# Feed-forward weights fetched one block in advance up to block 10, two from there on

## Chip, cores and metric

The kernel runs on one core of a Trainium2 chip. The metric is the device time of one execution in microseconds (us). The kernel before took 796.46 us (median of 3 runs, 795.83 to 797.32).

## What is computed

The input x has the shape (4, 1024, 256), in float32 as everything here. A transformer block is modulated by rows computed from a small conditioning input. First a gated linear recurrence takes the place of attention. Then a mixture of 8 experts follows, of which each token uses the best two:

```python
h = _layernorm(x) * (1 + ca) + sa
x = x + ga * attn(h)          # projections, sigmoid gates, a scan along the sequence, W_out
h = _layernorm(x) * (1 + cb) + sb
gate = softmax(h @ Wg + bg)   # 8 scores for each token; the two best, normalized
for e in range(8):
    y = gelu(h @ W1[e] + b1[e]) @ W2[e] + b2[e]
    output += y * combine_w[..., e]
x = x + gb * output
```

W1[e] is 256 x 1024 and W2[e] is 1024 x 256, so one expert's two matrices are 2 MB.

## The kernel before

**Chunks.** The first part runs over 8 chunks (NCH) of 512 tokens. In each, `project` (L417 for its matmuls) makes the four projections of one quarter of the hidden width, four times. Work of the neighbouring chunks is put between. A chunk's x1 is stored to the output (`o_resid`, L470), its second norm to a table `hx` in device memory (`f_store`, L498), and a swapped copy goes out and back for the router (`f_swap`, L518 and L525). For each batch of 1024 tokens the router ranks the tokens of every expert. `drain` (L586, on POOL) scatters (token, weight) pairs into `lists`, one region for each expert; a batch takes 16 scatters.

**Blocks.** The second part works through blocks of 256 entries of one expert. Which expert and which entries block j has is read from a small table computed on the chip (`entry`, L810). The table is made in three tiers. Blocks 0 to 7 (NE is 8) hold tokens of the first two batches, and blocks 8 to 15 (up to NM, 16) need three batches scattered. For each block there are these steps:

- `fetch_entries` (L822, on SP): 2 KB of the list, into `ent` (for the first 8 blocks `ente`).
- `fetch_rows` (L830, on POOL): two indirect gathers of 128 rows of `hx` each, into `hb`. They wait for the entries.
- `fetch_weights` (L852 to L855, on SP): four loads, which are w1 (1 MB), bb (4 KB), w2 (1 MB) and b2b (128 KB).
- `b_turn` (L911, on DVE): turns the rows into xT. Only for block 0 PE does it (L903), and this is put inside the last projection of the last chunk.
- `b_up` (L924, with the gelu on ACT, L933): 16 matmuls, which the trace shows as 32. `b_down` (L954): as many. DVE then adds the bias and multiplies (L968, L969), and POOL adds the rows to the output (L941).

**Buffers.** Weights have three places, used in turn: two sets of tiles, and for every third block the memory of the projection weights (`proj`, with b2b in `wo_sb`). So the weights of block j can start to load when block j - 3 is done with its own: w1 after its b_up, w2 after its b_down. Entries of block 8 and later have five places, and a place is free when its block's rows have been added to the output.

**Order.** The order on every engine is that of the program (a manual schedule); each engine runs ahead on its own until it meets a wait. All loads and stores of this part are issued by SP, one after another. SP waits at an instruction whose buffer is not free or whose data are not there, and everything behind it in the program waits too. So the place of a call in the program is a place in SP's queue.

**Where the change lies.** In the last chunk, after the second projection, the code calls `fetch_weights(0)`, `fetch_weights(1)`, then `fetch_entries` for blocks 0 to 7 (L1055 to L1063), and then on POOL the gathers of blocks 0 and 1. `fetch(j)` is called at the head of block j's work: L1116 for block 0, L1131 for block 1, L1160 for the later ones. It fetches entries of block j + 3 (from block 9 on), and rows and weights of block j + 2. The entries of the first block of a tier (8 and 16) are fetched two blocks in advance instead, and wait for all scatters of the batches in that tier (L1163). `fetch_used` does the same for the last blocks, of which the number is known only on the chip.

Of the kernel before, what the change touches and what calls it, by code (L numbers as in the profile page):

```python
# [19 lines left out]
def tile_adaln_block(  # L20
# [54 lines left out]
    NJ = (2 * T + E * (TK - 1)) // TK  # L75
# [3 lines left out]
    NE, EARLY_B, _ = TIERS[0]  # L79
# [48 lines left out]
    def load_x(c_: int, eng):  # L128
        xb = deep.tile([P, TPB, D], F32, tag="x", name=f"x_{c_}", bufs=5)
        b, i = divmod(c_, NB)  # L130
        src = x[b].rearrange("(n p) d -> p n d", p=P)
        eng.dma_start(out=xb, in_=src[:, ts(i, TPB), :])
        X[c_] = {"x": xb}
# [92 lines left out]
    def shift(c_):  # L226
        mv, rstd = X[c_]["stats"]
        nmr = small.tile([P, TPB], F32, tag="nmr", name=f"nmr_{c_}")
        X[c_]["nmr"] = nmr
        nc.vector.scalar_tensor_tensor(nmr, mv[:, :, 0], -1.0, rstd, ALU.mult, ALU.mult)  # L230
# [9 lines left out]
    def a_norm(c_):  # L240
        X[c_]["h"] = deep.tile([P, TPB, D], F32, tag="h", name=f"h_{c_}")
        norm(X[c_]["h"], c_)
# [116 lines left out]
    def a_mod(c_):  # L359
        h, md = X[c_]["h"], MDA[c_ // NB]  # L360
        nc.vector.tensor_mul(h, h, wide_row(md[:, 1, :]))
        nc.vector.tensor_add(h, h, wide_row(md[:, 0, :]))
# [112 lines left out]
    def f_stats(c_):  # L475
        X[c_]["stats"] = stats(X[c_]["x"], f"f{c_}")
# [105 lines left out]
    def drain(n: int):  # L582
        for _ in range(min(n, len(waiting))):
            nc.gpsimd.memset(between, 0.0)
            place, what = waiting.pop(0)
            ins = nc.gpsimd.indirect_dma_start(  # L586
                out=lists[:, :],
                out_offset=IndirectOffsetOnAxis(ap=place, axis=0),
                in_=what,
                in_offset=None,  # L590
                bounds_check=E * T - 1,
                oob_is_err=False,
            )

            for other in scattered:
                tc.declare_no_dep(ins.ins, other.ins, reason="other places")
            scattered.append(ins)
# [191 lines left out]
    def turns(pool, n: int, shape, dtype, tag: str, j: int):  # L789

        slots = kept.setdefault(tag, [None] * n)
        if slots[j % n] is None:
            slots[j % n] = pool.tile(shape, dtype, tag=f"{tag}{j % n}", name=f"{tag}_{j % n}", bufs=1)
        return slots[j % n]
# [6 lines left out]
    def seen(j: int):  # L801

        return next((batches * S for n, batches, _ in TIERS if j < n), T)

    def entry(j: int, row: int, most: int):
        which, i = next(
            ((w, j - n) for n, w in ((NM, "l"), (NE, "m"), (0, "e")) if j >= n)
        )
        what = tab[which]
        return nc.values_load(  # L810
            what[0:1, row, i : i + 1], engines=[SP], min_val=0, max_val=most,
            skip_runtime_bounds_check_because=why,
        )

    def fetch_entries(j: int):
        at = entry(j, 1, E * BPE)
        if j < NE:
            ent = xpool.tile([P, HK, 2], I32, tag=f"ente{j}", name=f"ente_{j}", bufs=1)
        else:
            ent = turns(xpool, 5, [P, HK, 2], I32, "ent", j)  # L820
        with nc.allow_non_contiguous_dma(reason="pairs of a list"):
            ld = nc.sync.dma_start(out=ent, in_=by_block[at])  # L822
        BK.setdefault(j, {}).update(ent=ent, ld=ld, gathers=[], acc=[])

    def fetch_rows(j: int, half: bool = False):

        hb = turns(xpool, 3, [P, HK, 2 * D], F32, "hb", j)
        for t in range(1 if half else HK):
            BK[j]["gathers"].append(
                nc.gpsimd.indirect_dma_start(  # L830
                    out=hb[:, t, :], out_offset=None, in_=hx[: seen(j), :],
                    in_offset=IndirectOffsetOnAxis(ap=BK[j]["ent"][:, t, 0:1], axis=0),
                    bounds_check=seen(j) - 1, oob_is_err=False,
                )
            )
        BK[j]["hb"] = hb

    def fetch_weights(j: int):
        if j >= NJ:
            return  # L840
        wpool = pools["w"]
        e = entry(j, 0, E - 1)
        if j % 3 == 2:
            w1 = proj[:, : KC * F].rearrange("p (k f) -> p k f", k=KC)
            w2 = proj[:, KC * F :].rearrange("p (c d) -> p c d", c=FC)
            b2b = wo_sb[:, 0, :]
        else:
            w1 = turns(wpool, 2, [P, KC, F], F32, "w1", j % 3)
            w2 = turns(wpool, 2, [P, FC, D], F32, "w2", j % 3)
            b2b = turns(wpool, 2, [P, D], F32, "b2b", j % 3)  # L850
        bb = turns(wpool, 3, [P, FC], F32, "bb", j)
        nc.sync.dma_start(out=w1, in_=W1r[e])  # L852
        nc.sync.dma_start(out=bb, in_=b1d[e])
        nc.sync.dma_start(out=w2, in_=W2r[e])
        nc.sync.dma_start(out=b2b, in_=b2[ds(e, 1), :].broadcast_to((P, D)))  # L855
        BK.setdefault(j, {}).update(w1=w1, w2=w2, bb=bb, b2b=b2b)
# [4 lines left out]
    def fetch(j: int):  # L861

        if j + 2 in firsts:
            fetch_entries(j + 2)
        if NE < j + 3 < NJ and j + 3 not in firsts:
            fetch_entries(j + 3)
        if j + 2 < NJ:
            fetch_rows(j + 2)
            fetch_weights(j + 2)

    def fetch_used(j: int, half: bool):
# [144 lines left out]
    for c_ in range(NCH):  # L1016
        nxt, prv, old = c_ + 1, c_ - 1, c_ - 2
        more, was, been = nxt < NCH, prv >= 0, old >= 0
        b, part = divmod(c_, NB)

        route = old // NB if been and old % NB == NB - 1 else None
        placed = (c_ - 3) // NB if c_ >= 3 and (c_ - 3) % NB == NB - 1 else None


        if c_ + 3 < NCH:
            load_x(c_ + 3, nc.sync)
        if more:
            shift(nxt)
        project(c_, 0, [lambda: a_norm(nxt)] if more else [])
        drain(6 if c_ + 2 >= NCH else 3)  # L1030
        if more:
            a_mod(nxt)
        if was:
            a_skip(c_)
            o_pe(prv)
            o_resid(prv)
        if placed is not None:
            r_second(placed)
        if part == NB - 1:
            load_mdf(b + 1)  # L1040


        if part == 0 and was:
            scale_out(b)
        if was:
            f_stats(prv)
        project(c_, 1, [lambda: a_square(nxt)] if more else [])
        if c_ == 0:
            first_contents()
        drain(6 if c_ + 2 >= NCH else 3)  # L1050
        if placed is not None:
            r_rank_pe(placed)
        if been:
            f_gate(old)
        if not more:  # L1055
            fetch_weights(0)
            fetch_weights(1)
            for j in range(NE):
                fetch_entries(j)

            wait_for(BK[0]["ld"], scattered)
            fetch_rows(0)
            fetch_rows(1)  # L1063
        if part == 0:
            if c_ == 0:
                setup_ctx.close()
                pools["w"] = ctx.enter_context(tc.tile_pool(name="weights", bufs=2))
            load_gb(b)
            load_mda(b + 1)
        elif c_ == 1:  # L1070
            clear_rows()
            if c_ == 0:
                load_mdf(1)


        if more:
            a_root(nxt)
        if was:
            shift(prv)
        if placed is not None:  # L1080
            r_place(placed)
        if route is not None:
            r_softmax(route)
        if more:
            a_scale(nxt)
        project(
            c_, 2,
            ([lambda: f_norm(prv)] if was else [])
            + ([lambda: r_exp(route)] if route is not None else []),
        )  # L1090
        drain(6 if c_ + 2 >= NCH else 3)
        if part == 0:
            store_gb(b)
        if c_ + 2 < NCH:
            a_stats(c_ + 2)


        if not was:
            a_skip(c_)
            scale_out(b)  # L1100
        if was:
            f_mod(prv)
            f_store(prv)
        project(c_, 3, [lambda: a_turn(nxt) if more else b_turn(0)])
        drain(6 if c_ + 2 >= NCH else 3)
        if was:
            f_swap(prv)
        if route is not None:
            r_first(route)
        if placed == EARLY_B - 1:  # L1110
            tab["e"] = full_table(NE, "e")
# [129 lines left out]
```

## Time and profile before

| | |
|---|---|
| median of 3 runs | 796.46 us |
| the profiled execution | 795.87 us, span 794.1 us |
| PE (TensorE matmul) busy | 773.7 us, 97% of the span |
| DVE (VectorE) busy | 504.7 us, 64% |
| POOL (GpSimd) busy | 292.7 us, 37% |
| ACT (ScalarE) busy | 242.1 us, 30% |
| DMA | 138.13 MB, mean 174 GB/s |
| granted TensorE clock, mean | 0.992 |

The profile is of one execution. Times in it count from the start of the span. PEld is the loading of weights into TensorE, which goes on beside the matmuls. Queue names with a q at the end (SPq, POOLq) are the engine's own instruction queue, in which it issues DMAs. "Idle before" is the time that an engine stood before an instruction, with what ended it. "To landing" is the time from a DMA's issue until its data are there.

From the span's start to about 308 us PE works on the projections, and from 308 us on it works on blocks, first mixed with the last work of the first part and from 347 us without it. The costliest groups of PE are those of the blocks:

```profile
L954 PE MATMUL pye_False<-w,g_False 128*128 128x256 f32 x672 | 148.7, 379 | 0.0
L924 PE MATMUL ph_False<-xT,w 128*128 128x256 f32 x672 | 148.6, 379 | 0.0
...
L924 PE MATMUL ph_False<-xT,proj 128*128 128x256 f32 x320 | 70.7, 379 | 0.0
L954 PE MATMUL pye_False<-proj,g_False 128*128 128x256 f32 x320 | 70.7, 379 | 0.0
```

One of these rows gives line, engine, operation, output and inputs, shape and count; after the bar come the busy us in all and the mean ns of one; after the next bar the idle us before them. The weights are moved by these issues (KB each, median us to landing):

```profile
w<-in_L_ffn_W_dram SPq DMA_DIRECT2D x48, 1024.0 KB, 7.0
proj<-in_L_ffn_W_dram SPq DMA_DIRECT2D x24, 1024.0 KB, 7.4
```

### The profile page before, as it was taken

Reading aid. Unit: us, or ns where it says so; the run is one execution under the profiler, and the core shown is the slowest. Engines: PE = TensorE matmul, PEld = TensorE weight load, DVE = VectorE, ACT = ScalarE, POOL = GpSimd, SP = SyncE. Lnnn points to the kernel's source line nnn. Section 1 sums busy time; section 2 is a strip of 40 time slices with the busy share of each in tenths; the row PEclk is TensorE's granted clock in tenths of the full one; section 3 lists DMA queues with packets and bytes.
Section 4 is the critical chain, followed back from the end, with each engine's and each line's share of the span. In section 5 each row is a group of like instructions: output and inputs, shape, how many; then the busy total and the mean of one; then the engine's idle time right before and its main releaser. Section 6 shows DMA issues by size and latency. Waiting matters only on the chain.

```text
span 794.1 us, 10809 instructions
## 1 busy us (share of the span) xinstructions
PE 773.7 (97%) x3279; PEld 578.1 (73%) x3279; DVE 504.7 (64%) x1391; ACT 242.1 (30%) x560; POOL 292.7 (37%) x370
## 2 busy tenths in 40 slices
PE   8999999999999987999999999999999999999995
PEld 5464545464555635888888888888888888888994
DVE  5787877899789955955645654453635454453564
ACT  4434243535344242132312222131222222132231
POOL 2103010106412812256646465543434343343431
PEclk9999999999999998999999999999999999999998
DMA  8411424052222385698839988797877777785781
GB/s 293 106 58 47 134 98 125 27 179 52 76 80 87 81 253 159 199 288 197 233 95 238 231 224 233 226 281 224 230 218 212 199 225 234 211 232 159 226 263 28
DMA packets 116040, 138.13 MB, mean 174 GB/s; under 512 B 25782, under 2 KB 100090, under 8 KB 115968
## 3 DMA queue, kind: packets, MB, share of 16 engines
q1 hardware_dynamic: 97184, 111.46, 44.5%
q0 software_dynamic: 17216, 25.25, 15.9%
q8 instruction: 32, 0.52, 0.3%
q10 hardware_dynamic: 1568, 0.57, 0.3%
q14 instruction: 40, 0.33, 0.2%
HBM read 113.52 MB, written 25.42 MB: 175 GB/s over the span
## 4 chain that ended last, share of the span: by engine, by line
PE 83%; DMA 9%; DVE 2%; issue 2%; SPq 2%; POOL 0%; POOLq 0%; ACT 0%; DVEq 0%
PE pye_False L954 24%; PE ph_False L924 23%; DMA hb<-hx,ent 7%; PE pya L454 7%; PE pu L417 7%; PE pk L417 6%; PE pgo L417 6%; PE pgi L417 6%; PE idle L263 1%; DMA out_dram<-yb_False,ent 1%; SPq L855 1%; PE pta L399 1%; PE pm L290 1%; DMA hb<-hx,ente 1%; PE pl L564 0%
## 5 line engine op out<-in xcount | busy, mean ns | idle before, releaser
L933 ACT ACTIVATE g_False<-ph_False,bb 128x256 f32<-128x256 f32 x248 | 104.0, 471 | 301.8 <-issue 205.3
L911 DVE STREAM_TRANSPOSE xT<-hb 32x128 f32<-32x128 f32 (+1 forms) x576 | 168.9, 293 | 13.3 <-DMA hb<-hx,ent 4.1
L954 PE MATMUL pye_False<-w,g_False 128*128 128x256 f32 x672 | 148.7, 379 | 0.0
L924 PE MATMUL ph_False<-xT,w 128*128 128x256 f32 x672 | 148.6, 379 | 0.0
L924 PEld LDWEIGHTS ph_False<-xT,w 128*128 128x128 f32 x672 | 127.5, 190 | 17.7 <-issue 0.5
L954 PEld LDWEIGHTS pye_False<-w,g_False 128*128 128x128 f32 x672 | 127.5, 190 | 17.7 <-ACT g_False L933 0.2
L941 POOL DMA_INDIRECT out_dram<-yb_False,ent x46 | 73.4, 1596 | 149.8 <-DVE yb_False L969 149.4
L968 DVE TENSOR_TENSOR yb_False<-pye_False,b2b 128x256 f32<-128x256 f32 x42 | 17.8, 424 | 126.2 <-PE pye_False L954 123.2
L586 POOL DMA_INDIRECT lists<-pay,placei x64 | 67.4, 1053 | 27.9 <-DMA ent<-lists 16.3
L924 PE MATMUL ph_False<-xT,proj 128*128 128x256 f32 x320 | 70.7, 379 | 0.0
L954 PE MATMUL pye_False<-proj,g_False 128*128 128x256 f32 x320 | 70.7, 379 | 0.0
L924 PEld LDWEIGHTS ph_False<-xT,proj 128*128 128x128 f32 x320 | 60.8, 190 | 8.3
L954 PEld LDWEIGHTS pye_False<-proj,g_False 128*128 128x128 f32 x320 | 60.8, 190 | 8.3
L830 POOL DMA_INDIRECT hb<-hx,ent x53 | 55.6, 1049 | 22.9 <-issue 20.9
L417 PE MATMUL pu<-hT,proj 128*128 128x512 f32 x128 | 61.9, 607 | 0.0
L417 PE MATMUL pk<-hT,proj 128*128 128x512 f32 x128 | 61.0, 599 | 0.7 <-ACT hT L1011 0.7
L417 PE MATMUL pgo<-hT,proj 128*128 128x512 f32 x128 | 60.2, 592 | 0.0
L417 PE MATMUL pgi<-hT,proj 128*128 128x512 f32 x128 | 60.1, 592 | 0.0
L223 POOL TENSOR_TENSOR rstd_f<-rstd_f,expo 128x4 f32<-128x4 f32 x8 | 8.2, 1023 | 135.9 <-DVE rstd_f L222 135.9
L454 PE MATMUL pya<-wo,z 128*128 128x256 f32 x256 | 56.6, 379 | 0.0
L454 PEld LDWEIGHTS pya<-wo,z 128*128 128x128 f32 x256 | 48.6, 190 | 9.5 <-issue 3.4
L417 PEld LDWEIGHTS pgo<-hT,proj 128*128 128x128 f32 x128 | 24.5, 191 | 31.2 <-issue 27.3
(234 smaller groups left out, 797.6 us busy)
## 6 DMA issues: line engine op xcount, KB each, us to landing
w<-in_L_ffn_W_dram SPq DMA_DIRECT2D x48, 1024.0 KB, 7.0
proj<-in_L_ffn_W_dram SPq DMA_DIRECT2D x24, 1024.0 KB, 7.4
hx<-gb SPq DMA_DIRECT2D x4, 1024.0 KB, 4.5
out_dram<-x SPq DMA_DIRECT2D x8, 512.0 KB, 3.2
hx<-h SPq DMA_DIRECT2D x8, 512.0 KB, 3.1
x<-in_L_attn_x_dram SPq DMA_DIRECT2D x7, 512.0 KB, 4.9
swapped<-u SPq DMA_DIRECT2D x7, 512.0 KB, 2.9
hT<-swapped SPq DMA_DIRECT2D x28, 128.0 KB, 2.6
```

The source lines that it names most:

```text
L223: nc.gpsimd.tensor_tensor(rstd, rstd, expo[:, 0, :], ALU.pow)
L263: nc.tensor.transpose(idle[:, :P], ident, ident)
L417: nc.tensor.matmul(ps, lhsT=w[:, k, col : col + P], rhs=hT[:, k, :], start=(k == 0), stop=(k == KC - 1),)
L454: nc.tensor.matmul(py[:, t, :], lhsT=z[hc][:, ts(2 * q + t, P)], rhs=wo[:, hc, :], start=(hc == 0), stop=(hc == HC - 1),)
L586: ins = nc.gpsimd.indirect_dma_start(out=lists[:, :], out_offset=IndirectOffsetOnAxis(ap=place, axis=0), in_=what, in_offset=None, bounds_ ...
L830: nc.gpsimd.indirect_dma_start(out=hb[:, t, :], out_offset=None, in_=hx[: seen(j), :], in_offset=IndirectOffsetOnAxis(ap=BK[j]["ent"][:, t ...
L911: nc.vector.transpose(to[ts(q, SQ), :, :, ts(i, SQ)], hb[ts(i, SQ), :, :, ts(q, SQ)])
L924: nc.tensor.matmul(ph[:, u, :], lhsT=w1[:, k, ts(fc, P)], rhs=xT[:, k, :n], start=(k == 0), stop=(k == KC - 1),)
L933: nc.scalar.activation(g[:, fc, :n], ph[:, u, :], AF.Gelu_apprx_tanh, bias=bb[:, fc : fc + 1])
L941: return nc.gpsimd.indirect_dma_start(out=out_rows[:n], out_offset=IndirectOffsetOnAxis(ap=at, axis=0), in_=yb, in_offset=None, bounds_che ...
L954: nc.tensor.matmul(py, lhsT=g[:, fc, ts(t, P)], rhs=w2[:, fc, :], start=(fc == 0), stop=(fc == FC - 1),)
L968: nc.vector.tensor_add(yb, py, b2b)
```

## The change

The weights of block 1 are no longer asked for in the last chunk. `fetch(j)` asks for the weights of block j + 1 up to j = 10 (NE + 2), and for those of block j + 2 from j = 10 on. So `fetch(0)` asks for block 1, `fetch(9)` for block 10, `fetch(10)` for blocks 11 and 12, and `fetch(11)` for block 13. Entries and rows are fetched as far in advance as before. The order of the calls within `fetch` stays: entries, rows, weights. Buffers, transfers and their number are the same. `fetch_used` is not touched.

```diff
@@ -866,6 +866,10 @@
             fetch_entries(j + 3)
         if j + 2 < NJ:
             fetch_rows(j + 2)
+
+        if j <= NE + 2:
+            fetch_weights(j + 1)
+        if NE + 2 <= j < NJ - 2:
             fetch_weights(j + 2)
 
     def fetch_used(j: int, half: bool):
@@ -1054,7 +1058,6 @@
             f_gate(old)
         if not more:
             fetch_weights(0)
-            fetch_weights(1)
             for j in range(NE):
                 fetch_entries(j)
 
```

## Prediction

> **What bounds the kernel now.** I read the shares of busy time first, then the idle time of PE by what ended it, then the stretches around the one long idle time, then SP's queue there. PE is busy for 773.7 of the 794.1 us, so only its idle time and its slow time can be won. The waits of PE name one idle time of any size:
>
> ```profile
> engine line waited for: us in total, times, longest us
> PE ptx L903 <- DMA hb<-hx,ente: 7.4, 1, 7.4
> PE idle L263 <- POOL ident masks.py:199: 1.5, 1, 1.5
> ```
>
> PE stands for 7.4 us before the four transposes of block 0 (L903), until the gather of that block's rows lands. The stretches before it, in it, from its end to the first product of block 0, and of that block follow (busy us of PE, PEld, DVE, ACT, POOL, then granted clock, DMA share, GB/s):
>
> ```profile
> 279.00:294.57 15.57, 15.57 (x51) 6.56 (x49) 7.84 (x15) 8.27 (x13) 1.04 (x1) 1.00 0.98 307
> 294.57:302.00 7.43, 0.00 (x1) 0.03 (x1) 2.29 (x2) 0.60 (x1) 4.63 (x4) 0.86 0.53 147
> 302.00:308.40 6.40, 6.30 (x13) 2.99 (x14) 2.07 (x3) 0.00 (x0) 2.02 (x2) 0.63 0.54 161
> 308.40:333.10 24.70, 23.80 (x128) 20.09 (x127) 22.21 (x77) 5.57 (x11) 2.15 (x3) 1.00 0.47 154
> ```
>
> The DMA engines are full (0.98) until just before the idle time, and after it the clock is only 0.63. What fills them is on SP's queue (start, us of the issue):
>
> ```profile
> 278.52 0.41 SPq L852 DMA_DIRECT2D w<-in_L_ffn_W_dram  x1
> ...
> 280.23 0.44 SPq L855 DMA_DIRECT2D b2b<-in_L_ffn_b_dram  x1
> 281.17 0.38 SPq L852 DMA_DIRECT2D w<-in_L_ffn_W_dram  x1
> ...
> 283.01 5.74 SPq L855 DMA_DIRECT2D b2b<-in_L_ffn_b_dram  x1
> 289.51 6.70 SPq L822 DMA_DIRECT2D ente<-lists  x8
> ```
>
> The four loads of block 0 go out, then the four of block 1, whose last issue is held for 5.74 us (others take 0.44), and only then the small lists of entries. The first list was issued at 289.51 and took 5.9 us to land (DMA to landing of that one row): 295.4. The first gather starts at 296.27, the second at 298.17 and lands 4.33 us later (chain of waits), 302.5. From list to rows is thus 7.1 us. The chain runs through exactly this: the held b2b issue, ente, hb, then ptx.
>
> **Part 1: the loads of block 1 leave the head of the queue.** On SP, one table read with its register steps and four DMAs (2.2 MB) go from ahead of the lists to behind them. The first list can then be issued at 280.67 (end of the b2b issue of block 0) plus 0.76 (what lay between the held issue's end, 288.75, and 289.51): 281.4. It still queues behind block 0's own weights. Their w2 was issued at 279.67 and took 8.6 us: 288.3; b2b lands 0.35 us behind w2 (the later group, issued at 318.15 and 318.71, landed after 7.5 and 7.3 us), and the list a few tenths on: 288.9 (estimate). Bounds: 287.7 if block 0's w2 takes the 7.5 us of that later group, 290 if the tiny packets cost a microsecond more. Rows land 7.1 us later, 296.0, or 295.3 if the second gather takes 3.6 us (the shortest of these gathers), the engines being free by then. I take 295.6. PE wants them at 294.57: 1.0 us of the wait stays and **6.4 us go** (bounds 5.3 and 7.4).
>
> The clock comes back with it. In the stretch after the wait pu's four matmuls took 3.41 us in the chain against 1.72 everywhere else: 1.69 lost, and the transposes lost 0.2 or so. The row says that a wait of 7.43 us costs about 1.9 us more; it can't say what one of 1.0 us costs. By proportion 0.26 us would stay. The Trainium skill ("TensorE: Matmul & The Clock Gate", Part 1) has the clock halved after an idle window of about 3.4 us, which would leave nothing of it at 1.0 us; in the trace the clock is 1.00 up to 299, 4.4 us into the wait. I take the rule: **1.9 us go** (1.6 by proportion).
>
> What is late next: DVE frees itself of the modulation (L488) at 296.9, so the copy of xT ends at 297.6 and the product with pu (L434) can follow pu's end at about 298.2. It started at 306.95, so DVE's chain, which is busy for 22.21 of the next 24.70 us, moves by 8.7 us, no less than PE. Nothing there holds back more than PE itself. Sum of part 1: 8.3 us (range 7.0 to 9.3).
>
> **Part 2: block 1's loads come at the head of block 0.** They take the place in SP's queue where block 2's stood, behind the swap of chunk 6 (L518, L525). Block 2's were issued from 316.95 and the last landed at 326.0; moved up by 8.3, block 1's are there by 317.7, and b_up(1) starts at 333.0 less 8.3, 324.7. Cover 7 us. Block 2's loads go behind the last stores of attention (L470, L498), where block 3's were at 333.67: 325.4 after the move, landing within some 9 us, while b_up(2) starts at 347.6 less 8.3, 339.3. Cover 5 us. No cost.
>
> **Part 3: blocks 3 to 6.** No list is fetched between these weights, so SP runs ahead of the program's order and each load waits, as now, for its buffer (L854 waits for L954 of the block three before). Same times relative to PE: nothing.
>
> **Part 4: blocks 7 to 11, the dear part.** From fetch(6) on, lists stand ahead of weights, and the list of block 8 waits for all scatters of three batches. SP's longest such wait is in this row:
>
> ```profile
> SPq L822 <- DMA lists<-pay,placei: 84.2, 10, 12.5
> ```
>
> Now block 7's weights were already issued (382.32 and 389.23); afterwards they stand where block 8's are now, and so on up to block 11:
>
> ```profile
> 409.55 1.54 SPq L822 DMA_DIRECT2D ent<-lists  x2
> 411.67 0.37 SPq L852 DMA_DIRECT2D proj<-in_L_ffn_W_dram  x1
> ...
> 423.67 0.37 SPq L822 DMA_DIRECT2D ent<-lists  x1
> 424.63 0.37 SPq L852 DMA_DIRECT2D w<-in_L_ffn_W_dram  x1
> ```
>
> The last scatter is paced by block 5's outputs, so these times move with PE. Time from the issue of w1 to the block that will want it: 411.67 to 417.33 (block 7), 5.7 us; 424.63 to 431.14, 6.5; 437.95 to 444.96, 7.0; 451.52 to 458.77, 7.3; 465.25 to about 472.6, 7.3. Time to landing in the same slots, the same gathers beside them: 5.0 in the first; in the second the small bb behind w1 lands at 425.24 + 5.9 = 431.1, so w1 takes 6.5 or less; 7.2 in the fourth; none is shown for the third and fifth. In the first:
>
> ```profile
> DMA to landing us min/median/max: 5.0/5.0/5.0
> ```
>
> So all just arrive. Here a rule of the Trainium skill speaks against the change: "DMA: Bandwidth & Descriptors", Bandwidth, Measured, gives 6.15 us for a transfer of 1 MB. By it block 7 waits 0.5 us and the others nothing; by the slot's own 5.0 us none waits. From both I take **0.5 us of loss in all** (bounds: 0, and 2.4 if every w1 takes 7.2 us: 1.5 + 0.7 + 0.2). w2 is wanted 6.9 us after w1 and lands 7 to 9 us after its own issue, 1.2 us behind w1's: on time.
>
> **Part 5: fetch(10) issues blocks 11 and 12 together**, 4.5 MB at 465.25. Block 12's is wanted at about 486.4, the extra 2.2 MB take some 7 us at the 307 GB/s of the full stretch above: no wait. From there on the queue is the same as now; the number of DMAs and bytes is unchanged, and PE, DVE, ACT and POOL keep their order. From 333 to the last block PE has no wait to absorb a shift, so the gain reaches the end.
>
> **Sum.** 6.4 + 1.9 - 0.5 = 7.8 us off the profiled execution's 795.87: 788.1. That execution lies 0.6 us under the median of the runs, 796.46, which gives 788.7. I say 788.3, and count the rivals from 796.2, the same middle.
>
> **Rivals.**
> 1. *Weights late at blocks 7 to 11, part of the gain back.* For: margins of a microsecond or less in five slots, 0.9 DMA share there. Against: the slots' own landings. At 7.2 us each 2.4 of the 8.3 us are lost: 790.3; at 8 us 2.3 + 1.5 + 1.0 + 0.7 + 0.7 = 6.2: 794.1.
> 2. *Slower: the same queue, each block waiting behind its list.* The gain of 8.3 is eaten when w1 takes about 8.4 us on average in the five slots. At 9.2 us (the row at 496.74) the losses are 3.5 + 2.7 + 2.2 + 1.9 + 1.9 = 12.2, 3.9 more than is won: 800. For: 9.2 and 11.3 us occur. Against: they occur where two blocks' weights are in flight at once, or other traffic is queued ahead; here one block's are. A late block also pushes PE but not the next list, which hangs on the block before.
> 3. *The rows remain late.* The list is behind block 0's weights anyway, and gathers may be slower. If half of the 6.4 stays and the clock still drops: 793. If all stays: 796.
>
> **How the numbers follow.** No change within 0.2% means 1.6 us here, about what a measurement of this kernel can tell. Forecast 0.60 (786.6 to 789.9); rival 1 0.18 (790 to 794.5); rival 3 in part 0.05, wholly 0.06; rival 2 0.11. The first, the second and half of rival 3 are faster: 0.83; same 0.06; slower 0.11. The range runs from 786.5 (no wait left at block 0, no late weights) to 794.0, leaving out rival 2 and the rest.
>
> **What would show it.** Lists issued near 281.5 and landed near 289; PE's wait at L903 about 1 us and the granted clock 1.00 after it; pu at 1.72 us; b_up(0) near 300. Right for part 4 if PE shows no wait for a weight above a microsecond at L924. Wrong if L924 waits for DMA w or proj in blocks 7 to 11 by some microseconds each, or if ptx still waits for hb beyond 297.

## The result and the profile after

The changed kernel takes 789.09 us (median of 4 runs, 788.57 to 790.33), beside 796.89 us for the kernel before: the ratio is 0.9893, 95% interval 0.986 to 0.9926. Measured again later, the ratio was 0.9905 (0.989 to 0.992). The span of the profiled execution (790.33 us) is 788.6 us.

These are the waits of PE in the changed kernel (us in all, times, longest). From L870 up to the removed call its lines stand four further down than in the kernel before: L907 is the old L903, L928 the old L924 and L958 the old L954.

```profile
PE ph_True L928 <- issue: 1.8, 2, 1.1
...
PE ptx L907 <- DMA hb<-hx,ente: 0.8, 1, 0.8
...
PE pye_False L958 <- DMA w<-in_L_ffn_W_dram: 0.7, 1, 0.7
...
PE ph_False L928 <- DMA proj<-in_L_ffn_W_dram: 0.3, 1, 0.3
```

The wait of 7.4 us for block 0's rows is down to 0.8. Two waits for weights are new. The first row belongs to the last short blocks (`ph_True`), which "The end" below takes up; "issue" is time in which PE waited for nothing that the profile shows. The stretches up to, in and behind that wait (columns as before: busy us of PE, PEld, DVE, ACT, POOL, then clock, DMA share, GB/s) show that the clock stays at 1.00, and that the DMA engines are no longer full ahead of it (0.74 instead of 0.98):

```profile
279.00:294.57 15.57, 15.49 (x52) 6.56 (x50) 8.37 (x20) 8.41 (x14) 4.75 (x5) 1.00 0.74 204
294.57:300.00 5.43, 4.74 (x16) 2.73 (x17) 5.00 (x6) 1.09 (x3) 3.77 (x3) 1.00 0.73 218
300.00:324.00 24.00, 23.08 (x125) 19.46 (x124) 21.52 (x78) 5.13 (x11) 2.15 (x3) 1.00 0.53 177
```

SP's queue there (start, us of the issues): the lists follow block 0's loads directly, and block 1's weights come 26 us later. Between the two is only the work of chunk 6 and its swap.

```profile
280.60 0.44 SPq L855 DMA_DIRECT2D b2b<-in_L_ffn_b_dram  x1
281.82 7.83 SPq L822 DMA_DIRECT2D ente<-lists  x8
...
307.64 0.40 SPq L852 DMA_DIRECT2D w<-in_L_ffn_W_dram  x1
```

What is lost again is seen on PE at blocks 7 and 8 (start, us), and in the chain of waits, where a DMA's row runs from its issue to its landing:

```profile
408.34 7.15 PE L928 MATMUL ph_False<-xT,w 128*128 128x256 f32 x32
416.15 7.15 PE L958 MATMUL pye_False<-w,g_False 128*128 128x256 f32 x32 [0.67 <-DMA w<-in_L_ffn_W_dram]
423.61 7.14 PE L928 MATMUL ph_False<-xT,proj 128*128 128x256 f32 x32 [0.31 <-DMA proj<-in_L_ffn_W_dram]
```

```profile
404.60 11.42 DMA w<-in_L_ffn_W_dram
...
418.52 4.95 DMA proj<-in_L_ffn_W_dram
```

A group of 32 matmuls without a wait gives way to the next after 6.91 us. From 408.34 to 416.15 are 7.81 us and from there to 423.61 are 7.46, so 0.90 and 0.55 us are lost; the start of block 7 came 0.31 us late as well. The second half of block 7's weights, issued at 404.60, took 11.42 us to land.

### The profile page after: what moved, and what is told of

Same layout as the page of the kernel before. It is cut to its first block, busy times and chain, and to the rows that moved or that the text cites. A ratio compares the mean times of both kernels' runs of the same rounds, so it can differ in the third digit from the quotient of the medians.

```text
span 788.6 us, 10806 instructions
## 1 busy us (share of the span) xinstructions
PE 771.8 (98%) x3279; PEld 576.2 (73%) x3279; DVE 504.5 (64%) x1391; ACT 241.8 (31%) x560; POOL 293.8 (37%) x370
## 4 chain that ended last, share of the span: by engine, by line
PE 81%; DMA 11%; DVE 2%; issue 2%; SPq 1%; POOL 1%; POOLq 0%; ACT 0%; DVEq 0%
PE ph_False L928 23%; PE pye_False L958 23%; PE pya L454 7%; PE pu L417 7%; PE pk L417 6%; PE pgi L417 6%; PE pgo L417 6%; DMA hb<-hx,ent 6%; DMA out_dram<-yb_False,ent 2%; DMA w<-in_L_ffn_W_dram 1%; PE pta L399 1%; PE pm L290 1%; DMA proj<-in_L_ffn_W_dram 1%; DMA wmod_sb<-in_L_wmod_dram 1%; DMA ente<-lists 0%
## 5 line engine op out<-in xcount | busy, mean ns | idle before, releaser
L958 PE MATMUL pye_False<-w,g_False 128*128 128x256 f32 x672 | 148.8, 379 | 0.7 <-DMA w<-in_L_ffn_W_dram 0.7
L928 PE MATMUL ph_False<-xT,w 128*128 128x256 f32 x672 | 148.6, 379 | 0.1
L958 PEld LDWEIGHTS pye_False<-w,g_False 128*128 128x128 f32 x672 | 127.4, 190 | 18.6 <-ACT g_False L937 1.2
L928 PEld LDWEIGHTS ph_False<-xT,w 128*128 128x128 f32 x672 | 127.5, 190 | 18.1 <-issue 1.0
L928 PE MATMUL ph_False<-xT,proj 128*128 128x256 f32 x320 | 70.8, 379 | 0.3 <-DMA proj<-in_L_ffn_W_dram 0.3
L958 PE MATMUL pye_False<-proj,g_False 128*128 128x256 f32 x320 | 70.7, 379 | 0.0
L928 PEld LDWEIGHTS ph_False<-xT,proj 128*128 128x128 f32 x320 | 60.7, 190 | 8.9 <-issue 0.7
L958 PEld LDWEIGHTS pye_False<-proj,g_False 128*128 128x128 f32 x320 | 60.8, 190 | 8.3
L417 PE MATMUL pu<-hT,proj 128*128 128x512 f32 x128 | 60.2, 592 | 0.0
L972 DVE TENSOR_TENSOR yb_False<-pye_False,wo_sb 128x256 f32<-128x256 f32 x20 | 8.5, 424 | 60.1 <-PE pye_False L958 60.1
```

What stands on the lines that cost most here:

```text
L417: nc.tensor.matmul(ps, lhsT=w[:, k, col : col + P], rhs=hT[:, k, :], start=(k == 0), stop=(k == KC - 1),)
L928: nc.tensor.matmul(ph[:, u, :], lhsT=w1[:, k, ts(fc, P)], rhs=xT[:, k, :n], start=(k == 0), stop=(k == KC - 1),)
L958: nc.tensor.matmul(py, lhsT=g[:, fc, ts(t, P)], rhs=w2[:, fc, :], start=(fc == 0), stop=(fc == FC - 1),)
L972: nc.vector.tensor_add(yb, py, b2b)
```

## The experiments

The starts of PE's groups divide every profiled execution into stretches. The table gives the start of block 0's first product, the time from the start of block 2 to that of block 9, and the time from the start of b_down of the last whole block to that of the last block ("end"). All are in us, from the traces of the kernels that follow, one profile each where no number is given.

| kernel | b_up(0) starts | block 2 to 9 | end |
|---|---|---|---|
| before (3 profiles) | 308.40, 308.65, 307.83 | 97.37, 97.36, 97.37 | 38.80, 39.21, 38.83 |
| changed (4 profiles) | 299.07, 299.38, 299.35, 299.50 | 99.20, 97.76, 97.36, 98.20 | 40.82, 41.13, 38.62, 39.09 |
| late weights alone | 309.43 | 98.58 | 39.05 |
| one in advance throughout | 299.31 | 97.79 | 39.36 |
| two in advance from block 2 | 299.24 | 97.36 | 40.13 |
| weights ahead of lists | 299.80 | 97.36 | 38.89 |
| first list first | 298.31 | 97.36 | 39.80 |
| only behind the lists | 303.85 | 97.36 | 39.17 |
| kept warm | 306.47 | 97.36 | 39.52 |

My theory was that the gain is the place of the lists in SP's queue and that the loss comes from weights standing behind lists that wait for scatters. The rivals are in the expectations.

**Two blocks in advance from block 2 on, block 1's weights still at the head of block 0** (against the changed kernel):

```diff
-        if j <= NE + 2:
-            fetch_weights(j + 1)
-        if NE + 2 <= j < NJ - 2:
+        if j == 0:
+            fetch_weights(1)
+        if j < NJ - 2:
             fetch_weights(j + 2)
```

> Block 1's weights at the head of block 0 as in the changed kernel, but block 2's right behind them and two blocks in advance from there on. Theory (the gain is the list's place in SP's queue, the loss is block 7 to 9's weights standing behind lists that wait for scatters): the wait before block 0's transposes stays near 0.8 us and the waits for weights in blocks 7 to 9 (1.9 us by the trace of the changed kernel) are gone, so some 1.9 us less than the changed kernel: 787.2 us, ratio to before 0.988. Rival (one block in advance is needed for the gain, since block 2's 2.2 MB would again stand in the way): block 0 or 1 wait for some microseconds and the time is 789 or more.

Measured: 787.23 us, ratio 0.9872 (0.9858 to 0.9886). The wait at block 0 is 0.7 us and no wait for weights is left. One block in advance is thus not needed for the gain; only the four loads of block 1 had to move. The intervals of this kernel and the changed one overlap, so it is the traces rather than the times that show the late weights gone.

**The other half alone:** block 1's weights stay ahead of the lists, and blocks 2 to 10 come one block in advance.

```diff
-        if j <= NE + 2:
+        if 1 <= j <= NE + 2:
             fetch_weights(j + 1)
...
             fetch_weights(0)
+            fetch_weights(1)
```

> The other half alone: block 1's weights ahead of the lists as in the kernel before, blocks 2 to 10 one block in advance. Theory: block 0 waits 7.4 us as before and blocks 7 to 9 lose some 1.9 us for weights: 798.8 us, ratio 1.002. Rival (the late weights cost nothing, the extra microseconds of the changed kernel are scatter of its tail): 796.9 us, ratio 1.000.

Measured: 797.70 us, ratio 1.0016 (1.0006 to 1.0025), so the late weights cost time of their own. Blocks 2 to 9 take 1.21 us longer, less than the 1.9 expected; PE waited 0.9 us for block 8's weights (`proj`) and not for block 7's. In the chain of waits w1 of block 8 takes 6.33 us to land:

```profile
426.68 6.33 DMA proj<-in_L_ffn_W_dram
433.01 0.14 issue
433.15 7.14 PE ph_False L928 x32
```

**Weights ahead of the lists**, still one block in advance:

```diff
     def fetch(j: int):
 
+        if j <= NE + 2:
+            fetch_weights(j + 1)
         if j + 2 in firsts:
...
-        if j <= NE + 2:
-            fetch_weights(j + 1)
```

> The changed kernel with the one-block-in-advance weights (blocks 1 to 11) ahead of the lists inside the fetch of a block instead of behind them. Theory (place in the queue): no wait for weights in blocks 7 to 9, 787.2 us, ratio 0.988. Rival (one block in advance is too late in itself): the waits in blocks 7 to 9 remain and the time is 789.1 us, ratio 0.990.

Measured: 787.97 us, ratio 0.9895 (0.9881 to 0.9909). By the time this can't be told from the rival. The one profile has 97.36 us for blocks 2 to 9 and no wait for a weight, which alone would not tell either, as one of the four profiles of the changed kernel has the same. The times of issue tell: w1 of block 8 was issued at 402.91, 19.7 us before the block began (422.56), where the changed kernel's first profile has 5.1 (418.52 to 423.61). The same weights, asked for in the same `fetch`, have a whole block more when they don't stand behind the list.

**Only behind the lists.** In the kernel before, block 1's weights move behind the eight lists, but stay in the last chunk:

```diff
             fetch_weights(0)
-            fetch_weights(1)
...
             fetch_rows(1)
+            fetch_weights(1)
```

> The kernel before with block 1's weights moved only behind the eight lists, still in the last chunk. Theory (queue place): the first list lands near 289 as in the changed kernel; the weights now run beside the gathers on the same 16 DMA engines, so the second gather takes longer than 4 us: wait of PE 1 to 3 us instead of 7.4, clock kept, no late weights later: 787 to 790 us, ratio 0.988 to 0.991. Rival (it is the 2.2 MB in flight and not their place that makes the rows late): the wait stays near 7 us and the time is 796 us.

Measured: 793.49 us, ratio 0.9951 (0.9938 to 0.9963). Neither forecast holds: the time is 3.5 us above the upper end of my theory's range. The first gather was issued at 290.38, as in the changed kernel (289.94), but PE got the rows at 296.62 and 298.34 instead of 295.26. The transposes of block 0 and the next matmuls on PE:

```profile
296.62 0.30 PE L903 MATMUL ptx<-ident,hb 128*128 128x128 f32 x1 [2.03 <-DMA hb<-hx,ente]
298.34 0.55 PE L903 MATMUL ptx<-ident,hb 128*128 128x128 f32 x3 [1.42 <-DMA hb<-hx,ente]
298.72 3.02 PE L417 MATMUL pu<-hT,proj 128*128 128x512 f32 x4
```

The two stretches from the wait on (columns as above):

```profile
294.60:298.90 4.30, 0.86 (x5) 0.70 (x6) 2.28 (x2) 0.60 (x1) 3.42 (x3) 1.00 1.06 377
298.90:303.90 5.00, 5.00 (x9) 1.98 (x9) 2.67 (x4) 0.00 (x0) 0.27 (x1) 0.66 0.97 323
```

The DMA engines are full with block 1's weights while the gathers run, the rows come 3 us later for it, and the clock falls after all. So in this profile the place behind the lists is worth 4.4 us at b_up(0) (308.3, the mean of three, to 303.85), and the later time of asking, when the gathers are over, another 4.5 (to 299.3, the mean of four). The profile is of the fastest of the five runs (791.28 us). By the medians the place is worth 3.5 us of the 9.8 that the kernel with two blocks in advance gains in the same round (797.02 to 793.49 and to 787.23). The theory was a third to a half of it.

**Kept warm.** In the kernel before, PE transposes a constant while it waits; the result is not used.

```diff
+        def kept_warm():
+            warm = ps_y.tile([P, TB], F32, tag="y", name="warm")
+            for _ in range(60):
+                nc.tensor.transpose(warm[:, :P], ident, ident)
+            b_turn(0)
...
-        project(c_, 3, [lambda: a_turn(nxt) if more else b_turn(0)])
+        project(c_, 3, [lambda: a_turn(nxt) if more else kept_warm()])
```

> The kernel before with 60 transposes of a constant (some 6.5 us at 0.109 us each) put on PE ahead of block 0's own, so that PE works through most of its wait. Theory (the wait costs 7.4 us and the fallen clock another 1.7 to 1.9): rows still land near 302.5, the clock stays 1.00, pu's matmuls take 1.72 us instead of 3.41 and b_up(0) starts some 1.9 us earlier: 795.1 us, ratio 0.9977. Rival (pu was slow for another reason, the copy of xT or the DMA traffic): 797.0 us, ratio 1.000.

Measured: 794.83 us, ratio 0.9986 (0.998 to 0.9993). PE there:

```profile
294.90 6.71 PE L1107 MATMUL warm<-ident 128*128 128x128 f32 x60
302.12 0.30 PE L903 MATMUL ptx<-ident,hb 128*128 128x128 f32 x1 [0.51 <-DMA hb<-hx,ente]
302.65 0.55 PE L903 MATMUL ptx<-ident,hb 128*128 128x128 f32 x3 [0.23 <-DMA hb<-hx,ente]
303.03 1.88 PE L417 MATMUL pu<-hT,proj 128*128 128x512 f32 x4
```

The row of the stretch from there on (columns as above) has the clock at 1.00:

```profile
302.50:307.00 4.50, 4.35 (x14) 2.39 (x15) 2.60 (x4) 0.27 (x1) 2.02 (x2) 1.00 0.68 223
```

The rows land when they did, and pu gives way to the next matmuls after 1.72 us (303.03 to 304.75): the clock was a cost of its own beside the wait. In the trace b_up(0) starts 1.8 us earlier. The median gained only 1.0 us, and the interval shuts out the 1.9 us expected. In the profile the end took 39.52 us, 0.6 more than the mean of the kernel before, which would account for most of the rest; why it did is open.

**The first list ahead of block 0's own weights too** (against the version with two blocks in advance):

```diff
-            fetch_weights(0)
-            for j in range(NE):
-                fetch_entries(j)
-
+            fetch_entries(0)
             wait_for(BK[0]["ld"], scattered)
+            fetch_weights(0)
+            for j in range(1, NE):
+                fetch_entries(j)
+
```

> The two-blocks-in-advance version that has block 1's weights at the head of block 0 (787.2 us), with the first list of block 0 ahead of block 0's own weights too. Theory (what is left of the wait, 0.7 us, is the list queueing behind block 0's weights): the first list lands near 284, the rows before PE wants them at 294.4, even if the weights beside them stretch the gathers to 8 us as when block 1's weights ran beside them; the weights of block 0 are there by 293: 786.5 us, ratio 0.987. Rival (block 0's weights, now behind the list's wait for the scatters, become the wait of b_up(0) at 299): 788 us or more.

Measured: 786.99 us, ratio 0.9883 (0.9868 to 0.9898), the same as without this step. The wait for the rows is gone and b_up(0) starts 0.9 us earlier, but the trace shows a new wait in the waits of PE, for DVE's chain, which had moved less than PE:

```profile
PE pr L673 <- DVE chose L640: 0.6, 1, 0.6
```

**One block in advance throughout:**

```diff
-        if j <= NE + 2:
+        end = (2 * T - E * P) // TK - 1
+        if j <= end:
             fetch_weights(j + 1)
-        if NE + 2 <= j < NJ - 2:
+        if j == end:
             fetch_weights(j + 2)
```

> Weights one block in advance not only up to block 10 but through all 28 blocks of fixed number. Theory (what counts is which wait stands ahead in SP's queue, not the number of blocks): from block 12 on a list waits only for the rows of the block two before to be added, and leaves the weights more than 15 us; at the next tier (block 16) the list was issued at 516.3 and block 15 starts at 527.8, so its weights have 9 us. No further loss: the time of the changed kernel, 789.1 us, ratio 0.990. Rival (one block in advance loses a little in each block): 18 blocks more at 0.3 to 0.6 us each, 794 us or more.

Measured: 788.16 us, ratio 0.9907 (0.9892 to 0.9922), no slower than the changed kernel. From block 12 on PE waits for no weight in its profile (its one wait for a weight, 0.3 us, is at block 9). So nothing here shows a cost of the number of blocks in advance by itself, and the rival falls.

**The changed kernel again:**

> The changed kernel once more beside the versions above, for the waits at blocks 7 to 9 and at the last short blocks. Theory: 789.1 us, waits for weights in blocks 7 to 9 of 1 to 2 us in all, in which block they fall varies from run to run. Rival (they were one run's accident): no wait there and 787.2 us.

Measured: 788.71 us, ratio 0.9905. Blocks 2 to 9 took 97.76 us, so the loss was 0.4 us this time: less than the 1 to 2 us of my theory, more than the rival's none.

**The end.** In the first two profiles of the changed kernel the last short blocks took some 2 us longer than before, so both kernels were profiled twice more.

> The kernel before, looked at again for its last short blocks: from the start of the last whole block's second half (b_down) to that of the last block took 38.8 us in its first profile. Theory (this stretch scatters from execution to execution in any kernel, with the landing of the gathers and of the added rows): 38.8 to 41.2 us, as in all kernels seen. Rival (the changed kernel's end is slower in itself): 38.8 to 39.2 again.

> The changed kernel, looked at again for the same stretch, 40.8 and 41.1 us in its two profiles. Theory (scatter): anywhere from 38.8 to 41.2 us. Rival (slower in itself): 40.5 us or more. For blocks 2 to 9 (97.4 us without a late weight) both expect 97.5 to 99.2 us.

> The kernel before once more, for the same stretch. Theory: 38.8 to 41.2 us. Rival: 38.8 to 39.2 us.

> The changed kernel once more, for the same stretch. Theory: 38.8 to 41.2 us. Rival: 40.5 us or more.

Measured: 39.21 and 38.83 us before, 38.62 and 39.09 after (one run each: 797.00, 795.37; 786.62, 788.80 us). The changed kernel also has the shortest end of all profiles, just under the range forecast, so it need not be slower there. On average it was: 39.9 us in four profiles beside 38.9 in three. Whether this is chance or comes of the change, so few profiles don't show, and what makes the end vary by up to 2.5 us was not looked into. For blocks 2 to 9 the first of these two profiles of the changed kernel, with 97.36, lies below both forecasts: there was no loss at all.

## Why the prediction was right, point by point

**What bounds the kernel: right.** One wait of PE, with the clock's fall, held what could be won. That the gain in the median, 7.8 us, is exactly the 7.8 us of the sum is luck. By the profiles' means 9.0 us were won at block 0, 0.9 lost by blocks 7 to 11 and 1.0 in the end, where the prediction had put nothing: 7.1 us, as the mean spans have it too (794.2 to 787.1). The parts too small and too large nearly cancel.

**Part 1, right in mechanism, a little too small: 8.3 us forecast, 9.0 measured** at b_up(0) (means 308.3 and 299.3). The list was issued at 281.82 (forecast 281.4), rows came at 295.26 (295.6), and 0.8 us of wait stayed (1.0). The term that was too small is that of the transposes. From the end of the wait to b_up(0) were 6.40 us before and 3.81 after (295.26 to 299.07); pu accounts for 1.69 of the 2.59, and the transposes for 0.9 where I had 0.2. One of the four was done ahead of the wait, as it needs only the first gather, and the other three took 0.55 us instead of 1.45 for all. That nothing of the clock's fall stays after a short wait, the rule of the Trainium skill ("TensorE: Matmul & The Clock Gate", Part 1) that I took over the proportion, holds for it: 1.00 in the stretch behind it. It does not cover two short waits close together, as the kernel with the loads only behind the lists showed.

**Part 2, right.** Block 1's weights were issued from 307.64 and block 2's from 324.01, and neither block waits.

**Part 3, right.** From block 2 to block 7 every kernel takes 69.7 us, and only the changed one's first profile shows 0.3 more, which is block 7's late start.

**Part 4, right in mechanism and place, and mis-sized.** Forecast 0.5 us for w1 being late; measured 1.8, 0.4, 0.0 and 0.8 us between blocks 2 and 9 in the four profiles, and 1.2 in the kernel with this half alone. The term that was off in all five is the slot of block 8, from the issue of its w1 to the end of the matmuls before it: 6.5 us forecast, 4.5, 5.4, 5.6, 5.6 and 5.4 measured. The list ahead of it came 6.3 to 7.4 us after the last scatter was issued (410.13 to 417.57 in the first profile), and 5.3 in the kernel before (418.42 to 423.67); why is open. In four of the five block 8 was late by 0.3 to 1.1 us. (In the fourth profile of the changed kernel the trace puts this wait down to an instruction of DVE, which elsewhere ended after block 8 had begun; that it was w1 is likely, not shown.) Two more terms were off in the first profile. The list of block 8 came 7.3 us after block 6 began, against 6.1 before (401.45 less 394.13; 409.55 less 403.43), because the last scatter that it waits for released SP some 4.5 us after its issue (396.83 to 401.3) instead of 3.2 (406.14 to 409.3); the slot of block 7 shrank from 5.7 to 4.8 us (403.26 to 408.03, the end of block 6's matmuls). And w2 I had landing in 7 to 9 us and on time: it took 11.42. As to w1, the row of 5.0 us was nearer than the 6.15 us of the Trainium skill ("DMA: Bandwidth & Descriptors", Bandwidth, Measured) in the first profile: 4.95 us at block 8, and at block 7 no more than 5.1 (issued at 403.26, the block began at 408.34). In the kernel with this half alone it was 6.33, so neither figure holds for every execution; and by the section's heading its figure is for loads issued from GpSimd, while SP issues these.

**Part 5 and the rest, nearly right.** Blocks 11 and 12, asked for together, held nothing up in three profiles. In the fourth w1 of block 11, issued at 455.55, took 9.5 us to land, and the block was 0.6 us late:

```profile
465.14 7.14 PE L928 MATMUL ph_False<-xT,proj 128*128 128x256 f32 x32 [0.44 <-DMA proj<-in_L_ffn_W_dram]
```

The gain of block 0 reaches block 9 whole where no weight is late (97.36 us from block 2 in six kernels). From block 9 to the last whole block three profiles of the changed kernel show under 0.1 us of difference and the fourth 0.7, nearly all of it at block 11.

**Rivals.** The weights' lateness was there and gave back a tenth of the gain (0.9 us as the mean of the four, block 11 with it, of 9.0), well short of the 2.4 us from which the first rival began; the slower rival's 8.2 us never came near. The third fell with the list's landing.

## What to carry to other kernels

In a queue that issues in order, look at what stands ahead of the small transfer that starts a chain: here 2.2 MB for a later block held up 2 KB for the next one, and moving them was worth 1% where the engine's share of busy time had said 97%. Moving a load behind the small one is only part of it if the load then runs beside the gathers that follow; ask for it when those are over. And a load put behind a wait of the same queue inherits that wait: place it ahead of the wait, or check the slot to the microsecond, over several profiles, as what is waited for varies (here 3.0 to 4.6 us from one scatter's issue to that of the list behind it, 6.3 to 7.4 for the next).

## What the hardware showed that I had not expected

- Two waits of 2.0 and 1.4 us with a single transpose of 0.30 us between them brought the granted clock down to 0.66 over the next 5 us, though each was much shorter than the 7.4 us of the kernel before (0.63 over 6.4 us). A single wait of 0.8 us left it at 1.00.
- With one block's weights in SP's queue, and gathers and the adding of rows on the same DMA engines, w1 of block 7 (1 MB) landed after some 5 us and w2 (1 MB), issued 1.3 us behind it, after 11.4. The engines had moved most of the bytes by 412.5 (360 GB/s from 405 to 412, 127 from 412.5 to 416), and the load still counted as landed only at 416.0. The engines were full to the end (share 1.18 from 412.5 to 416): of the 0.44 MB of that stretch 0.37 belonged to POOL's transfers. That these held back the last part of w2 is likely, not shown.
